# Block 0 of a two-block hybrid network as interleaved streams of steps, with a gathered top-1 FFN and a factored state-space decay

## The chip, the cores and the metric

One NeuronCore of a Trainium2 chip runs the whole network in one launch. The metric is the device time of a launch in microseconds (us), lower is better. The engines are PE (TensorE, matrix products, with PEld its weight loads), DVE (VectorE), ACT (ScalarE), POOL (GpSimd) and SP (SyncE, which only issues DMAs here). Every engine takes its instructions strictly in order; a DMA is issued by SP, ACT or POOL. All arithmetic is in fp32.

## The reference

The input is x, 4 sequences of 256 tokens with 256 features. Each of eight sub-layers adds to it:

```python
x = x + shift(layernorm(x))       # block 0, attention a: token shift, WKV recurrence
x = x + ffn0(layernorm(x))        # top-1 of 8 experts, 256 -> 256, with bias
x = x + ssm(layernorm(x))         # block 0, attention b: gated state space, 8 heads
x = x + ffn0(layernorm(x))        # the same weights again
x = x + attn_a(layernorm(x))      # block 1: grouped attention, 16 heads
x = x + ffn1(layernorm(x))        # top-4 of 32 experts, gated, inner width 96
x = x + attn_b(layernorm(x))      # the same with distance bias
x = x + ffn1(layernorm(x))
```

- shift mixes each token with the one before it in three ways (for k, v and r), projects each mix, runs the recurrences `a = e1*a + e2*v` and `b = e1*b + e2` over time, and projects `(a/b)*r`.
- ffn0 takes, for each token, the softmax over 8 router logits, the expert with the largest probability (the first one at a tie), and adds `prob * (W[expert] x + b[expert])`.
- ssm projects to gates, values h, B, C and step sizes dt, runs a causal convolution of width 4, and computes for each head `y[l] = sum over s<=l of (C[l].B[s]) * exp(sum of A*dt over s+1..l) * dt[s]*h[s]`, plus `D*h`; then the gate, a root-mean-square norm and an output projection. The kernels compute the sum over a whole sequence at once rather than in the reference's chunks.

## The kernel before

The 1024 tokens are two groups of 512 (two sequences each); a group is four tiles of 128 tokens, kept in SBUF as `x[g]`. Block 0 and block 1 are written differently.

**Block 0** is four plain functions called in turn: `l0_attn_a` (lines 155 to 233), `l0_ffn`, `l0_attn_b`, `l0_ffn`. Here the compiler's own scheduler orders the instructions of each engine. Each function goes over both groups before the next begins.

- `l0_attn_a`: for each group the norm, then three mixes (ACT L181, DVE L183). For each half e of the features: products pk, pv, pr; `top` and `low` (L206, L208) with their exponentials; four scans (L220, L222); a reciprocal of the denominator (DVE, `rb`, L225) and a multiply on POOL (L226); then the output products `po_a`, added to x.
- `l0_ffn` is dense. All eight experts are computed for all tokens and weighted by `comb`, which is zero but for the chosen one:

```python
for t in range(NT):
    for pr in range(E0 // 2):
        pe = mm_tile(...)
        project(pe, lambda c: xnT[:, c, t*P:(t+1)*P], lambda c: W[:, c, pr*512:(pr+1)*512])
        for h in range(2):     # x += pe[expert] * comb[expert], DVE L284
            ...
```

- `l0_attn_b`: projections and convolutions of both groups first (`pcv`, `pg`, `pd`), then the step sizes, then per group and sequence b eight heads. For each head POOL multiplies a triangular mask by `A*dt` (`au`, L394 and L396). PE sums it along time for three 128x128 blocks (`pS`, L400 to L402: the two diagonal blocks of the sequence and the block below them), ACT takes the exponential `L`, DVE multiplies by the masked `C.B` (`Gm`), and three products with the values give `pY` (L383 to L387). After the eight heads follows the tail of the sequence: add (`yf`, DVE L415), gate (POOL L417), squares, transposes `pyt`, output products `pob`, add to x.

**Block 1** is a dictionary of streams, each a Python generator that emits instructions and yields `(cost, wait)`. The function `weave` (L450) keeps a planner's clock, and always takes the next step of the ready stream with the lowest rank; a stream may name others that must have ended, and how long ago. It runs inside `tc.manual_schedule()`, so the order written is the order each engine gets. Its stream `a0` is the first attention of group 0, `a1` that of group 1; `r0`, `e0`, `c0` route, run the experts and combine. Routing sends normalised rows to slots in a DRAM buffer `sent` by indirect DMAs on POOL (L807); the experts fetch it tile by tile (SP), write `done` (SP), and the combine gathers rows back by indirect DMA (POOL, L890).

**Loads.** SP loads x of both groups, then all weights of block 0 and the attention weights of block 1. ACT loads the small ones, and writes zeros (`nil`) to `sent` and `done` (20 DMAs of 512 KB, L988 and L992). `negA`, an exponential of an input vector, is ACT's first computation (L293). After block 0 its weight pool closes; the FFN weights `gu` and `dw` of block 1 go to the same memory (issued from 369 us on), and constants of block 1's attention are built on POOL and DVE there (L1008 to L1068).

PSUM has eight banks: three "mm", two "st", two "sq", one "acc". In block 0 general products take turns on "mm" and "st"; in block 1 on "mm" alone.

Of the kernel before, what the change touches and what calls it, by code (L numbers as in the profile page):

```python
# [9 lines left out]
F32 = mybir.dt.float32  # L10
I32 = mybir.dt.int32
# [19 lines left out]
NH, HP, NS = 8, 64, 64  # L31
DI = NH * HP
# [5 lines left out]
def two_blocks(ctx: ExitStack, tc: tile.TileContext, a: dict, out: bass.AP):  # L38
# [33 lines left out]
    for g in range(NG):  # L72
        xg = const.tile([P, NT, D], F32, tag=f"x{g}", name=f"x{g}")
        for t in range(NT):
            nc.sync.dma_start(xg[:, t, :], xin[g, :, t, :])
        x.append(xg)

    ident = const.tile([P, P], F32, tag="ident", name="ident")
# [13 lines left out]
    for g in range(NG):  # L92
# [3 lines left out]
        sent_to.append(dram_disjoint_views(sent[g], NT * TOPK))  # L96

# [57 lines left out]
    def l0_attn_a(pool, wpool):  # L155
        wk, wv, wr, wo = (
            load(n, [P, NC, D], wpool, nc.scalar if i % 2 else nc.sync)
            for i, n in enumerate(("L0a_Wk", "L0a_Wv", "L0a_Wr", "L0a_Wo")))
        tm = vec[:, :, 0:3]
        bk, bv, br, u, w = (vec[:, :, i] for i in range(3, 8))  # L160
        omt = const.tile([P, NC, 3], F32, tag="omt", name="omt")
        nc.vector.tensor_scalar(omt, tm, -1.0, 1.0, ALU.mult, ALU.add)
        bku = const.tile([P, NC], F32, tag="bku", name="bku")
        nc.vector.tensor_tensor(bku, bk, u, ALU.add)
        bkuw = const.tile([P, NC], F32, tag="bkuw", name="bkuw")
        nc.vector.tensor_tensor(bkuw, bku, w, ALU.subtract)
        negw = const.tile([P, NC], F32, tag="negw", name="negw")
        nc.vector.tensor_scalar(negw, w, -1.0, None, ALU.mult)

        mixed = []  # L170
        for g in range(NG):
            xp = pool.tile([P, NC, 2, S + 1], F32, tag="xp", name=f"xp_{g}")
            nc.gpsimd.memset(xp[:, :, :, 0:1], 0.0)
            layernorm_T(g, f"a0_{g}", lambda c: xp[:, c, :, 1:S + 1])
            add_row(g, bo0)
            mix = []
            for j in range(3):
                m = pool.tile([P, NC, 2, S], F32, tag=f"mix{j}", name=f"mix{j}_{g}")
                for c in range(NC):
                    tmp = pool.tile([P, 2, S], F32, tag="mixtmp", name=f"mixtmp_{g}_{j}_{c}")  # L180
                    nc.scalar.activation(  # L181
# [1022 lines left out]
```

## Time and profile before

| | us |
|---|---|
| median of 14 runs (lowest, highest) | 1018.68 (1013.98, 1022.24) |
| the profiled execution | 1023.53 |
| its span, first to last instruction | 1021.8 |
| busy in the span: PE, PEld, DVE, ACT, POOL | 822.4, 509.4, 528.3, 251.8, 280.1 |
| shift stage of both groups ends at | 83 |
| first ffn0 ends at | 152 |
| ssm ends at | 300 |
| second ffn0 ends at | 370 |
| attention a of group 0 ends at | 459 |
| last product; last write | 988; 1022 |

All times are microseconds from the span's start. The groups of the profile give line, engine, operation, output<-inputs, shapes and count, then busy time and mean nanoseconds of one, then idle time of the engine just before them and what ended it. An fp32 product appears as two PE records, so x256 means 128 products. The granted clock is the share of full speed that PE was allowed.

### The profile page before, as it was taken

To read this page: it belongs to the slowest core of one execution; us is meant where nothing else is said; L and a number is where in the kernel's file an instruction comes from. 1 tells how busy PE (TensorE), PEld (TensorE's weight loads), DVE (VectorE), ACT (ScalarE), POOL (GpSimd) and SP (SyncE) were. 2 spreads that over 40 slices of the span, in tenths; PEclk is the share of its full clock that TensorE was granted. 3 is DMA by queue.
4 is the path that set the end of the run, shared out by engine and by line. 5 is a ranking of instruction groups with operands and counts; after the bars stand their busy time and mean duration, and the time that the engine had idled before them with its cause. 6 is when DMAs were issued, how large, how long until landed. Compare 5 with 4: busy or idle time off the path is not lost.

```text
span 1021.8 us, 10802 instructions
## 1 busy us (share of the span) xinstructions
PE 822.4 (80%) x3464; PEld 509.4 (50%) x3464; DVE 528.3 (52%) x1570; ACT 251.8 (25%) x470; POOL 280.1 (27%) x344
## 2 busy tenths in 40 slices
PE   3468999988889968888899776978888899776960
PEld 2234444577674434334337665854334337665850
DVE  5886665835336664526635423545736535423532
ACT  3410006722220002321235111212232234111210
POOL 3100000376530040020360324116220360324105
PEclk8688999998789978977799968988998799978995
DMA  8750000000000057000024435532000023435633
GB/s 281 271 185 1 1 0 1 1 1 1 1 1 0 1 159 213 1 0 21 32 81 116 144 105 184 165 114 62 11 1 0 32 80 96 145 113 173 188 110 99
DMA packets 61551, 81.49 MB, mean 80 GB/s; under 512 B 5928, under 2 KB 52528, under 8 KB 60976
## 3 DMA queue, kind: packets, MB, share of 16 engines
q1 hardware_dynamic: 43760, 52.48, 16.7%
q0 software_dynamic: 6144, 16.79, 5.2%
q10 hardware_dynamic: 11584, 11.46, 3.2%
q8 instruction: 30, 0.49, 0.2%
q14 instruction: 33, 0.27, 0.1%
HBM read 42.96 MB, written 37.75 MB: 79 GB/s over the span
## 4 chain that ended last, share of the span: by engine, by line
PE 59%; DVE 15%; issue 12%; POOL 6%; DMA 4%; ACT 2%; another core or an unknown queue 2%; POOLq 0%; ACTq 0%; SPq 0%; DVEq 0%
PE pe_f L142 11%; PE pgu_f L142 7%; PE py_f L865 3%; PE pST_a L601 3%; PE pS_a L559 3%; PE pcv L142 2%; PE pST_b L601 2%; PE pob L142 2%; DVE junk_a L570 2%; PE pS_b L559 2%; PE po_a L142 2%; DVE ye_f L873 2%; DVE junk_b L570 2%; POOL yb_f L890 2%
## 5 line engine op out<-in xcount | busy, mean ns | idle before, releaser
L142 PE MATMUL pgu_f<-gu,xT_f 128*128 128x192 f32 x512 | 109.9, 363 | 9.4 <-DVE ye_f L873 4.9
L142 PE MATMUL pe_f<-L0f_W_sb,xnT_f 128*128 128x512 f32 x256 | 115.7, 600 | 0.0
L142 PEld LDWEIGHTS pgu_f<-gu,xT_f 128*128 128x128 f32 x512 | 91.3, 208 | 21.0 <-DVE ye_f L873 17.1
L890 POOL DMA_INDIRECT yb_f<-done,bk_f x64 | 67.0, 1047 | 122.2 <-DMA xe_f<-sent 48.0
L807 POOL DMA_INDIRECT sent<-xn_f,to_f x64 | 63.0, 985 | 72.6 <-DVE full L794 55.4
L284 DVE SCALAR_TENSOR_TENSOR x<-pe_f,comb_f,x 128x256 f32<-128x256 f32 x128 | 61.9, 484 | 39.6 <-PE pe_f L142 36.2
L865 PE MATMUL py_f<-dw,hT_f 96*128 96x256 f32 x256 | 71.8, 407 | 3.4 <-issue 1.8
L142 PEld LDWEIGHTS pe_f<-L0f_W_sb,xnT_f 128*128 128x128 f32 x256 | 46.6, 190 | 53.9 <-issue 51.6
L869 DVE TENSOR_TENSOR he_f<-he_f,pgu_f 128x192 f32<-128x192 f32 x64 | 22.5, 352 | 83.7 <-ACT he_f L859 72.9
L570 DVE CUSTOM_DVE_ANT_0 junk_a<-pS_a,tri 128x128 f32<-128x128 f32 (+1 forms) x128 | 45.8, 358 | 33.1 <-PE pS_a L559 26.5
L570 DVE CUSTOM_DVE_ANT_0 junk_b<-pS_b,tri 128x128 f32<-128x128 f32 (+1 forms) x128 | 45.8, 358 | 29.6 <-PE pS_b L559 23.0
L842 ACT COPY xT_f<-px_f 128x512 f32<-128x512 f32 x64 | 37.2, 585 | 89.3 <-PE px_f L839 72.1
L873 DVE COPY ye_f<-py_f 128x512 f32<-128x512 f32 x64 | 44.2, 691 | 21.4 <-PE py_f L865 7.1
L865 PEld LDWEIGHTS py_f<-dw,hT_f 96*128 96x128 f32 x256 | 49.9, 204 | 10.5 <-issue 2.3
L839 PE MATMUL px_f<-ident,xe_f 128*128 128x128 f32 x256 | 42.2, 294 | 12.3 <-DMA xe_f<-sent 10.1
L859 ACT ACTIVATE he_f<-pgu_f 128x192 f32<-128x192 f32 x64 | 21.1, 330 | 119.4 <-PE pgu_f L142 82.0
L881 DVE SCALAR_TENSOR_TENSOR x<-yb_f,wt_f,x 128x256 f32<-128x256 f32 x64 | 30.9, 484 | 37.3 <-DMA yb_f<-done,bk_f 37.1
L394 POOL TENSOR_SCALAR au<-m,dtad 128x256 f32<-128x256 f32 x32 | 31.0, 968 | 63.6 <-DVE dtad L350 38.3
L848 PE MATMUL ph_f<-ident,he_f 128*96 128x128 f32 x128 | 26.6, 291 | 26.9 <-DVE he_f L869 24.5
L608 POOL TENSOR_SCALAR_AFFINE_SELECT pT_a<-pT_a 128x512 f32<-128x512 f32 x32 | 19.7, 637 | 94.8 <-ACT pT_a L606 94.4
L839 PEld LDWEIGHTS px_f<-ident,xe_f 128*128 128x128 f32 x256 | 34.3, 153 | 22.6 <-issue 13.1
L606 ACT ACTIVATE pT_a<-pST_a 128x512 f32<-128x512 f32 x48 | 26.5, 595 | 73.0 <-PE pST_a L601 72.0
(297 smaller groups left out, 1456.0 us busy)
## 6 DMA issues: line engine op xcount, KB each, us to landing
xe_f<-sent SPq DMA_DIRECT2D x64, 256.0 KB, 2.7
done<-ye_f SPq DMA_DIRECT2D x64, 256.0 KB, 2.1
sent<-nil ACTq DMA_DIRECT2D x18, 512.0 KB, 3.1
gu<-in_L1f_gate SPq DMA_DIRECT2D x4, 768.0 KB, 18.1
gu<-in_L1f_up SPq DMA_DIRECT2D x4, 768.0 KB
dw<-in_L1f_down SPq DMA_DIRECT2D x4, 768.0 KB
L0f_W_sb<-in_L0f_W SPq DMA_DIRECT2D x4, 512.0 KB, 7.8
L0b_in_sb<-in_L0b_in SPq DMA_DIRECT2D x1, 1160.0 KB
```

Of the source, the lines that this page charges most:

```text
L142: nc.tensor.matmul(dst, w(c), rhs(c), start=(c == 0), stop=(c == n - 1))
L284: nc.vector.scalar_tensor_tensor(x[g][:, t, :], pe[:, h * D:(h + 1) * D], comb[:, t, e:e + 1], x[g][:, t, :], ALU.mult, ALU.add)
L394: nc.gpsimd.tensor_scalar(au[:, :S], m384[:, :S], ad[:, 2 * b, h:h + 1], None, ALU.mult)
L559: nc.tensor.matmul(both[r][:, at:at + 2 * w].rearrange("p (s k) -> p s k", s=2), qT[rows, c, q0:q0 + P], kb[rows, 2 * r:2 * r + 2, b * S:b ...
L570: nc.vector.tensor_tensor_reduce(out=junk[:, :w], in0=both[r][:, at:at + w], in1=tri[:, S - w:], scale=1.0, scalar=NEG, op0=ALU.add, op1=A ...
L601: nc.tensor.matmul(pS, kb[rows, s, k0:k0 + P], qm[rows].rearrange("p c q -> p (c q)"), start=True, stop=True)
L807: nc.gpsimd.indirect_dma_start(out=sent_to[g][t * TOPK + j], out_offset=bass.IndirectOffsetOnAxis(ap=to[:, t, j:j + 1], axis=0), in_=xn[:, ...
L839: nc.tensor.transpose(px[:, j * P:(j + 1) * P], xe[q][:, k, c * P:(c + 1) * P], ident)
L842: nc.scalar.copy(xT[q].rearrange("p k c t -> p (k c t)"), px)
L865: nc.tensor.matmul(py[:, k * D:(k + 1) * D], hT[q][:, k, :], dw[:, 2 * q + k, :], start=True, stop=True)
L873: nc.vector.tensor_copy(ye.rearrange("p k d -> p (k d)"), py)
L890: nc.gpsimd.indirect_dma_start(out=yb, out_offset=None, in_=done[g], in_offset=bass.IndirectOffsetOnAxis(ap=back[:, t, j:j + 1], axis=0), ...
```

## The change

Block 0 is rewritten as streams too, and the whole kernel runs under `tc.manual_schedule()` with one planner clock. All its general products now use the three "mm" banks.

**Streams.** A is the shift stage of a group, R a route, X the fetch of extra experts' weights, E the experts, C the combine, S the state space; T, Y, G, D are R, X, E, C of the second FFN. The number is the rank, the last dictionary says after which streams, and how long after:

```diff
+        streams = {
+            "A0": (2, shift_mix(0, a0, shift), {}),
+            "A1": (3, shift_mix(1, a0, shift), {}),
+            "R0": (0, first_route("f00", 0, f0, first, ways0[0]), {"A0": 0.5}),
+            "R1": (0, first_route("f00", 1, f0, first, ways0[0]), {"A1": 0.5}),
+            "E0": (1, first_experts("f00", 0, f0, W, bias, eb, ways0[0]), {"R0": 1.5}),
+            "E1": (1, first_experts("f00", 1, f0, W, bias, eb, ways0[0]), {"R1": 1.5, "E0": 0.0}),
+            "X0": (0, first_extra("f00", 0, f0, first, ways0[0]), {"R0": 0.0}),
+            "X1": (0, first_extra("f00", 1, f0, first, ways0[0]), {"R1": 0.0}),
+            "C0": (0, first_combine("f00", 0, f0, ways0[0]), {"E0": 3.0}),
+            "C1": (0, first_combine("f00", 1, f0, ways0[0]), {"E1": 3.0}),
+            "fix": (0, second_fix(), {"A0": 0.0}),
+        }
+        weave(streams, ("A0", "A1"))
...
+            "S0": (4, state_space(0, b0, space), {"C0": 0.5}),
+            "S1": (5, state_space(1, b0, space), {"C1": 0.5, "S0": 0.0}),
+            "T0": (0, first_route("f01", 0, f0, first, ways0[1]), {"S0": 0.5}),
+            "G0": (1, first_experts("f01", 0, f0, W, bias, eb, ways0[1]), {"T0": 1.5, "E1": 0.0}),
+            "Y0": (0, first_extra("f01", 0, f0, first, ways0[1]), {"T0": 0.0}),
+            "D0": (0, first_combine("f01", 0, f0, ways0[1]), {"G0": 3.0}),
+        weave(streams, ("S1", "fix"))
...
+            "T1": (0, first_route("f01", 1, f0, first, ways0[1]), {"S1": 0.5}),
+            "G1": (1, first_experts("f01", 1, f0, W, bias, eb, ways0[1]), {"T1": 1.5, "G0": 0.0}),
+            "Y1": (0, first_extra("f01", 1, f0, first, ways0[1]), {"T1": 0.0}),
+            "D1": (0, first_combine("f01", 1, f0, ways0[1]), {"G1": 3.0}),
+            "a0": (2, attention("a1", 0, *attn_a), {"D0": 0.5}),
+        weave(streams, ("D1",))
+        early0.close()
+        w1 = ctx.enter_context(tc.tile_pool(name="w1", bufs=1, side="right"))
...                          # loads of gu and dw; then the streams of block 1 as before
+            "na": (3, norm_steps(1, "a1_1", early[0]), {"D1": 0.5}),
```

`weave(left, until)` keeps its clock between calls and stops when the named streams have ended. The pool `b0` of the state space takes the memory of the shift stage; `gu` and `dw` take that of block 0's weights.

**The FFN on slots.** Each expert has 128 slots per group, and three further tiles of 128 take the overflow of whichever experts have more than 128 tokens: 11 tiles. `first_route` computes router logits, the chosen expert, each token's rank within it (by products with triangular and all-ones matrices), then the slot on DVE in some 30 small operations, and scatters four tiles of rows:

```diff
+        for t in range(NT):
+            nc.gpsimd.indirect_dma_start(
+                out=first_to[g][t],
+                out_offset=bass.IndirectOffsetOnAxis(ap=to[:, t:t + 1], axis=0),
+                in_=xn[:, t, :], in_offset=None, bounds_check=EXTRA + 3 * P - 1,
+                oob_is_err=False)
+            yield 0.0, 1.28
```

`first_extra` finds which experts own the three extra tiles, and gathers their weights by six indirect DMAs (128 rows of 1 KB each). `first_experts` goes over six pairs of tiles, the last with one:

```diff
+                px = mm_tile(f"px_{name}_{i}")
+                for j in range(k * NC):
+                    nc.tensor.transpose(
+                        px[:, j * P:(j + 1) * P],
+                        xe[i][:, j // NC, (j % NC) * P:(j % NC + 1) * P], ident)
...
+                nc.scalar.copy(
+                    xT[i][:, :k].rearrange("p k c t -> p (k c t)"), px[:, :k * NC * P])
...
+                if q < 4:
+                    for j, e in enumerate(pairs[q]):
+                        project(py[:, j * D:(j + 1) * D], lambda c: xT[q][:, j, c, :],
+                                lambda c: W[:, c, e * D:(e + 1) * D])
+                    nc.vector.tensor_tensor(
+                        yf_, py[:, :k * D], bias[:, 2 * q * D:(2 * q + k) * D], ALU.add)
+                else:                # extra tiles: bias by a product with "chose", weights xw
...
+                    nc.scalar.copy(yf_, py[:, :k * D])
+                nc.sync.dma_start(first_done[g][...], ye[:, :k])
```

`first_combine` gathers four tiles of rows from `first_done` by indirect DMA on POOL and adds them to x with the gate, four DVE operations.

**The state space.** One generator per group. The two diagonal blocks keep masked sums, exponentials and products, now two heads at a time; the block below them is split into a factor of the earlier half (`reach[:, t]`, applied to the values: `left`) and one of the later half (`reach[:, NT + 2b + 1]`, applied to the product):

```diff
+            pS = mm_tile(f"pS_{g}_{b}_{h}")
+            nc.tensor.matmul(pS, strict, au.pop(k).rearrange("p h i l -> p (h i l)"),
+                             start=True, stop=True)
...
+            for h in (h0, h0 + 1):
+                hs = slice(h * HP, (h + 1) * HP)
+                for i in range(2):
+                    nc.tensor.matmul(pY[b][i][:, hs], L[k][:, h - h0, i, :],
+                                     hdt[2 * b + i][:, h, :], start=True, stop=True)
...
+        def between(b):
+            pO = bank("acc", f"pO_{g}_{b}")
+            nc.tensor.matmul(pO, Gm[b][:, 1, :], left[b].rearrange("p h q -> p (h q)"),
+                             start=True, stop=True)
```

The eight jobs (two sequences, four pairs of heads) form one loop; the gate, transposes and output products of sequence 0 are steps put between the jobs of sequence 1.

**The shift stage.** The same operations as steps; the scans of the denominator come before those of the numerator, and the output factor pr comes after both halves.

**Start and constants.** SP loads x of group 0, two weights, then x of group 1. On ACT, ahead of its first computation, come two zero fills of the slot buffers (1.44 MB each) and a broadcast of the expert biases (1 MB); DVE's multiply of `negA` is written ahead of all norms:

```diff
+        for g in range(NG):
+            nc.scalar.dma_start(
+                first_sent[g].rearrange("(p k) d -> p k d", k=E0 + 3),
+                nil.unsqueeze(1).to_broadcast([P, E0 + 3, D]))
...
+        nc.scalar.dma_start(
+            bias, a["L0f_b"].rearrange("e d -> (e d)").partition_broadcast(P))
...
+        nc.scalar.activation(negA, alog, AF.Exp)
+        nc.vector.tensor_scalar(negA, negA, -1.0, None, ALU.mult)
```

`second_fix` is a stream of rank 0: the 20 zero fills for block 1, one step each, and the constants of its attention, after A0. The loads of `gu` and `dw` are issued after D1's last step.

## The prediction

> **What bounds the kernel now.** I read the page's strip, then a table of stages, then the chain of the worst stages. A row is start:end, its length, busy us of PE, PEld, DVE, ACT and POOL, granted clock, DMA share, GB/s. In order: shift stage, first FFN, state space (two halves), second FFN, first attention of group 0.
>
> ```profile
> 12.00:83.00 71.00, 43.26 (x98) 24.24 (x99) 55.08 (x82) 21.91 (x30) 13.73 (x14) 0.74 0.65 228
> 83.00:152.00 69.00, 68.52 (x203) 32.09 (x202) 44.11 (x119) 3.75 (x8) 2.02 (x2) 1.00 0.00 0
> 152.00:197.00 45.00, 42.83 (x133) 20.17 (x132) 29.74 (x58) 29.90 (x45) 5.03 (x7) 0.96 0.00 1
> 197.00:300.00 103.00, 88.99 (x527) 78.15 (x526) 45.16 (x97) 32.15 (x71) 60.80 (x72) 0.85 0.00 1
> 300.00:370.00 70.00, 68.01 (x201) 31.61 (x198) 44.17 (x119) 3.75 (x8) 3.33 (x9) 1.00 0.00 1
> 370.00:459.00 89.00, 73.20 (x269) 33.85 (x270) 40.37 (x165) 22.87 (x42) 21.78 (x47) 0.81 0.37 107
> ```
>
> Both FFNs are pure PE at full clock. The shift stage is DVE (55 of 71). The state space has PE 89 of 103 busy at clock 0.85, so it has holes; its chain of waits shows where:
>
> ```profile
> 275.82 0.43 PE pob L142 x2
> ...
> 288.74 0.22 PE pY L387 x2
> ...
> 289.32 0.70 DVE yf L415
> 290.10 2.50 POOL yf L417 x2
> 292.64 1.54 PE pyt L430 x6
> 294.18 5.83 PE pob L142 x16
> ```
>
> Eight heads run from 277.1 to 289.3; then a serial tail to 300.0 costs 10.7 us, and the same matmul that took 0.43 a pair at 275.8 now takes 5.83/8 = 0.73, the PE having idled. There are four such tails. The costly groups:
>
> ```profile
> L142 PE MATMUL pe_f<-L0f_W_sb,xnT_f 128*128 128x512 f32 x256 | 115.7, 600 | 0.0
> L225 DVE RECIPROCAL rb<-sb 128x512 f32<-128x512 f32 x4 | 13.4, 3349 | 0.1
> L890 POOL DMA_INDIRECT yb_f<-done,bk_f x64 | 67.0, 1047 | 122.2 <-DMA xe_f<-sent 48.0
> ```
>
> Block 0 ends near 370; group 0's first attention ends at 459; 1021.8 - 459 = 563 us follow. The planner emits that remainder in the same order of steps before and after, so I carry 563 over and price the road to "a0 ends".
>
> **Start.** The shift's first normalised tile is written at 11.68. Its timeline (start, duration):
>
> ```profile
> 9.53 0.44 ACTq L65 DMA_DIRECT2D L0b_norm_sb<-in_L0b_norm  x1
> 9.99 1.28 ACT L293 ACT_TABLE_LOAD   x1 [9.99 <-DMA L0f_wg_sb<-in_L0f_wg]
> 11.29 0.21 ACT L293 ACTIVATE negA<-row 128x8 f32<-128x8 f32 x1
> ```
>
> ACT reaches that exponential only after issuing its DMAs. The change puts three large ones ahead of it (two zero fills of 1.44 MB, one bias broadcast of 1 MB), and, the order being manual, the DVE's negA multiply now stands ahead of both groups' statistics. Issue of one existing 512 KB zero fill costs 0.52 to 1.25, mean 1.06 in a burst of five. New issue time: at least 3x0.52 = 1.6, at most 2x2.75x1.25+1 = 8; I take 6, by the burst. So negA is done at 17.5; eight pairs of statistics (0.42+0.18, 4.6 together) then give the first normalised tile at about 22 (18 to 26): +10. Group 1's x moves behind two weight loads on SP; they issue in 0.33 each and x is wanted only at 20: nothing.
>
> **Shift stage.** Same operations. DVE from there: 8 norms 3.3, mixes 10.5, top/low 6.1, scans 11.6, ev 3, reciprocals 13.4, yT 3, output adds 3.4 = 54; plus group 0's routing, norm 4.2 and some 30 tiny ones at 0.16 = 5. The first 8.3 us (norm to first projection) hold 5 of DVE work, and group 0's chain runs nearly alone, with some 7 of exposed waits: 54+9+3+7 = 73, I take 74 (68 to 78). Group 1's shift ends at 96, its routing of group 0 with it.
>
> **FFN.** Removed: 137 us of dense PE. Added per group and pass: 11 tiles of two transposes (0.60 per four, so 0.30) and two 256-column products (0.44 each at full clock, as in py x4 at 0.88) = 13, plus three small bias products 1.3: 14.3; transposes, logits and rank products 1.2+1.9+1 = 4. Four times 18.3 is 73: PE work falls by 64. But each pass is now a chain through DRAM: scatter, fetch, products, store, gather. Indirect DMAs step at 1.28 to 1.31 on POOL; a fetch lands in 2.7, a store in 2.1, a gather in 3.3 to 3.6.
>
> First pass, between the stages: group 1's statistics end at 98.4; the planner puts its rsqrt (1.05) before group 0's fourth scatter, which issues at 100.6 and lands at 103 (2.5, between store and gather); the fetch lands at 106. Products 14.3, plus 4.5 for group 1's logits and ranks among them: 125; store 128.5; four gathers alternating with group 1's weight gathers, all queued on POOL: 138.5. Group 1 scatters until 121.5, fetches by 127, multiplies until 146. State space of group 0 is queued on DVE behind group 1's evictions (141), and its norm takes 6.4; its first PE work comes at about 150. So 54 us here (46 to 62) against 69: group 0's add is hardly hidden, since S0 waits for C0.
>
> **State space.** Per group: projections and convolutions 45/2 = 22.5. Per head before: 1.55 (pS 0.94, pY 0.61). After, two heads share one 512-column product (0.88) and need four pY (0.88): 1.76, eight times 14.1 against 24.8. Added: one 512-column product per sequence (1.8) and 0.4 of decay products; unchanged pG 1.7, transposes 1.8. First sequence's tail now lies among the heads: 3.5+1.2 of PE. Filling the first heads 3, last tail 10.7. Sum 22.5+14.1+2.2+3.5+4.7+3+10.7 = 61 (56 to 66). POOL's masked products fall from 32x(0.97+0.66) = 52 to about 16x1.26 = 20, the row of the 128x512 gate multiply; it no longer binds. S1 cannot start before S0 ends; its norm exposes 7. Beside S1 lies group 0's second pass: 18.3 of PE, its waits hidden by S1's convolutions. 150+61+7+61+18 = 297.
>
> **a0.** Norm 7: the constants that kept POOL busy and held rstd_a until 375 are built earlier, a gain of 4.5. From pk (381.4) to 458.9 it took 77.5, and group 1's second pass adds 18.3: 297+7+78+18 = 400 (390 to 412). The load of gu and dw (9.4 MB at 285 to 303 GB/s, 32 us) now waits for D1, around 370, and is first used some 80 us later: nothing, but up to 32 if that cover went. The other twenty zero fills take ACT 13 to 25 us of issue, covered by its slack (85 busy of 370).
>
> **Stalls.** 56 indirect DMAs are new. During such a burst of 16, engines stop on something that is not a kernel operation:
>
> ```profile
> ACT he_f L859 <- remote: 6.4, 1, 6.4
> ```
>
> I see about 10 us lost in that burst, 5 in the next: 0.3 to 0.6 each would be 17 to 34, but those were denser and beside 16 fetches; bounds 0 to 20, I take 8. a0 ends at 408.
>
> [...]
>
> [...]
>
> **Sum.** 408+563 = 971 span, plus the 1.7 by which this execution (1023.5) exceeded its span: 973. The median of the runs is 4.9 under that execution, so I expect 968; against 1018.7 that is -50.
>
> **Rivals.**
> *The chains are not hidden.* All engines run the planner's fixed order, so a gather or fetch that lands later than planned blocks PE, DVE or POOL with state-space or attention work behind it. For: ACT and DVE stopping 4 to 6 us in the burst. Against: 23 us of convolutions to hide under. If both second passes expose a chain like the first's group 0 (106 to 138 plus routing, some 30 us each, 60 for both), 968+60 = 1028. It decides from 50 us of exposed waits on.
> *Fewer waits than I gave.* The start isn't held (-8), stalls are 0 (-8), the first pass takes 46 (-8) and the state space 56 twice (-10): 934. For: PE-dense parts run at 1.00. Against: the shift's clock of 0.74.
> *The overlap exists in the order of issue only:* S0 waits for group 1's evictions and for its buffers, S1 for S0, so the groups still follow one another. Most of this is already in my sum; another 7 to 10 us at both handovers and 62 in the first pass: 968+26 = 994.
>
> **How the numbers follow.** Forecast (950 to 985) 0.45; fewer waits (below 950) 0.20; partial overlap (985 to 1016) 0.22; chains exposed (above 1020) 0.11; between them 0.02. Range 928 to 1012: below it lies 0.07 and above it 0.13. A measurement can tell 0.2% from no change, so 1016.6 to 1020.7 is "same". Faster 0.87, same 0.02, slower 0.11.
>
> **What would show it.** First xn at 22 and not 12; pe_f gone, py/px groups of 44 tiles in all; PE busy near 740; S0's first product near 150; two tails of about 10 us rather than four; a0 ending near 408 with the same 563 behind it. I am wrong if PE has idle stretches above 10 us ended by a DMA inside S1 or a0, if the first pass exceeds 62, or if the remainder changes its length.

## The result: slower by 0.9%, and the profile after

The changed kernel takes 1027.67 us (median of 10 runs, 1021.23 to 1031.40) against 1017.99 for the kernel before: a ratio of 1.0093, 95% interval 1.0077 to 1.0109. The forecast was 968 us. The page of its profiled execution:

```profile
span 1027.4 us, 10502 instructions
...
PE 762.2 (74%) x3264; PEld 488.1 (48%) x3264; DVE 501.3 (49%) x1556; ACT 257.4 (25%) x481; POOL 312.1 (30%) x361
...
PE 45%; issue 21%; DVE 15%; DMA 6%; POOL 5%; ACT 3%; another core or an unknown queue 3%; SPq 0%; POOLq 0%; ACTq 0%; DVEq 0%
```

PE is busy 60 us less than before (762 against 822), as a gain of the size forecast would need, and the span is longer all the same. The stages, in the columns of the first table above (start, the first FFN pass, state space of group 0, then group 1's with the second pass of group 0, attention of group 0 with the second pass of group 1, the remainder):

```profile
0.00:33.00 33.00, 0.00 (x0) 0.00 (x0) 5.43 (x30) 1.49 (x2) 4.80 (x25) 1.00 0.95 345
33.00:122.00 89.00, 52.28 (x126) 27.66 (x126) 61.55 (x109) 23.53 (x33) 15.81 (x11) 0.77 0.18 61
122.00:181.00 59.00, 42.92 (x183) 33.30 (x183) 20.66 (x79) 10.64 (x21) 23.62 (x23) 0.77 0.68 222
181.00:251.00 70.00, 57.28 (x216) 34.60 (x216) 40.17 (x71) 25.62 (x48) 29.96 (x51) 0.88 0.11 34
251.00:375.00 124.00, 95.87 (x359) 65.52 (x360) 63.78 (x157) 34.46 (x64) 39.36 (x35) 0.79 0.12 39
375.00:469.00 94.00, 81.96 (x338) 41.43 (x337) 45.52 (x202) 25.78 (x49) 27.67 (x32) 0.92 0.50 151
469.00:1027.00 558.00, 431.90 (x2046) 285.63 (x2044) 264.19 (x912) 135.83 (x265) 170.88 (x184) 0.87 0.30 95
```

Up to the end of the first attention PE works 330 us (second to sixth row); the rows of before gave 385 from 12 to 459. So 55 us of work are gone, but PE's idle time in that stretch rose from 74 (12 of the start included) to 139. The remainder is 558 us against the 563 that I carried over. The whole question is where 65 us of new idle time come from.

The start shows at once. ACT's own instructions there:

```profile
5.90 4.55 ACTq L1203 DMA_DIRECT2D fsent<-nil  x2
13.38 0.57 ACTq L66 DMA_DIRECT2D L0f_wg_sb<-in_L0f_wg  x1
14.42 1.18 ACTq L66 DMA_DIRECT2D L0f_b_sb<-in_L0f_b  x1
18.72 0.36 ACTq L1209 DMA_DIRECT2D bias<-in_L0f_b  x1
26.08 0.33 ACTq L66 DMA_DIRECT2D L0b_conv_sb<-in_L0b_conv  x1
26.45 0.44 ACTq L66 DMA_DIRECT2D L0b_norm_sb<-in_L0b_norm  x1
26.93 1.28 ACT L1271 ACT_TABLE_LOAD   x1 [26.93 <-DMA fsent<-nil]
28.22 0.21 ACT L1271 ACTIVATE negA<-row 128x8 f32<-128x8 f32 x1
```

The two zero fills cost 4.55 to issue, within my bounds. But between the end of one issue and the start of the next ACT then stands 2.9, 0.5, 3.1 and 7.0 us, 13.5 in all, and the profile ends this idle time with the DMA `fsent<-nil`. In these 33 us the DMA engines are nearly always busy (first row of the table: share 0.95, 345 GB/s). The exponential comes at 28.2 instead of 11.3. On DVE the multiply of `negA` starts at 28.46, after 23.85 us of waiting for it, and the first statistics, written behind it, at 28.55; the first normalised tile at 33.2.

The FFN's products on PE, all four passes (busy us, mean ns of one):

```profile
L150 PE MATMUL py_f<-L0f_W_sb,xT_f 128*128 128x256 f32 x128 | 36.2, 434 | 1.0 <-ACT xT_f L468 1.0
...
L464 PE MATMUL px_f<-ident,xe_f 128*128 128x128 f32 x88 | 16.4, 324 | 14.6 <-DMA xe_f<-fsent 10.9 <-issue 2.1 <-DVE x L512 1.6
...
L150 PE MATMUL pl_f<-L0f_wg_sb,xnT_f 128*128 128x8 f32 x64 | 13.9, 355 | 0.6 <-ACT xnT_f L215 0.6
L490 PE MATMUL py_f<-xw_f,xT_f 128*128 128x256 f32 x48 | 13.6, 405 | 0.0
...
L210 PE MATMUL pt_f<-ident,xn_f 128*128 128x128 f32 x32 | 9.5, 449 | 15.9 <-DVE xn_f L202 15.0 <-DVE low L273 0.9
...
L487 PE MATMUL py_f<-L0f_b_sb,chose_f 8*128 8x256 f32 x24 | 8.3, 426 | 0.0
```

py and px come to 74.5, or 18.6 a pass, where I had 14.3; logits, transposes and 5.4 of rank products to 28.8, or 7.2, where I had 4. A pass is 25.8 us of PE work on average instead of 18.3; with overlapping records counted once, the two first passes have 26.1 each, the second pass of group 0 25.7 and that of group 1 22.6.

### The profile page after: what moved, and what is told of

Read it like the earlier page. It is cut to its first block, busy times and chain, and to the rows that moved or that the text cites. A ratio compares the mean times of both kernels' runs of the same rounds, so it can differ in the third digit from the quotient of the medians.

```text
span 1027.4 us, 10502 instructions
## 1 busy us (share of the span) xinstructions
PE 762.2 (74%) x3264; PEld 488.1 (48%) x3264; DVE 501.3 (49%) x1556; ACT 257.4 (25%) x481; POOL 312.1 (30%) x361
## 4 chain that ended last, share of the span: by engine, by line
PE 45%; issue 21%; DVE 15%; DMA 6%; POOL 5%; ACT 3%; another core or an unknown queue 3%; SPq 0%; POOLq 0%; ACTq 0%; DVEq 0%
PE pgu_f L150 6%; PE py_f L150 3%; PE py_f L1111 3%; PE pST_a L847 3%; PE pS_a L805 2%; DVE junk_a L816 2%; PE pST_b L847 2%; DVE cv L537 2%; PE pS_b L805 2%; DVE ye_f L1119 2%; PE pob L150 2%; DVE junk_b L816 2%; DMA fsent<-nil 2%; PE pq_a L150 1%
## 5 line engine op out<-in xcount | busy, mean ns | idle before, releaser
L150 PEld LDWEIGHTS pgu_f<-gu,xT_f 128*128 128x128 f32 x512 | 89.8, 205 | 19.9 <-DVE ye_f L1119 16.1
L1115 DVE TENSOR_TENSOR he_f<-he_f,pgu_f 128x192 f32<-128x192 f32 x64 | 22.5, 352 | 87.6 <-ACT he_f L1105 76.2
L1111 PEld LDWEIGHTS py_f<-dw,hT_f 96*128 96x128 f32 x256 | 49.5, 203 | 13.3 <-issue 3.5
L852 ACT ACTIVATE pT_b<-pST_b 128x512 f32<-128x512 f32 x48 | 26.3, 595 | 73.0 <-PE pST_b L847 72.3
L847 PE MATMUL pST_a<-qm_a,kb_a 64*128 64x512 f32 x96 | 34.2, 693 | 8.1 <-DVE qm_a L832 5.3
L847 PE MATMUL pST_b<-qm_b,kb_b 64*128 64x512 f32 x96 | 34.8, 714 | 6.2 <-DVE qm_b L832 3.4
L805 PE MATMUL pS_b<-kb_b,qT_b 64*128 64x256 f32 (+1 forms) x128 | 36.6, 594 | 3.5 <-DVE nmx L816 3.4
L210 PE MATMUL pt_a<-ident,xn_a 128*128 128x128 f32 x32 | 8.6, 423 | 40.6 <-DVE xn_a L202 40.6
```

The source lines that it names most:

```text
L150: nc.tensor.matmul(dst, w(c), rhs(c), start=(c == 0), stop=(c == n - 1))
L805: nc.tensor.matmul(both[r][:, at:at + 2 * w].rearrange("p (s k) -> p s k", s=2), qT[rows, c, q0:q0 + P], kb[rows, 2 * r:2 * r + 2, b * S:b ...
L847: nc.tensor.matmul(pS, kb[rows, s, k0:k0 + P], qm[rows].rearrange("p c q -> p (c q)"), start=True, stop=True)
L852: nc.scalar.activation(pT.rearrange("p c q -> p (c q)"), pS, AF.Exp)
L1111: nc.tensor.matmul(py[:, k * D:(k + 1) * D], hT[q][:, k, :], dw[:, 2 * q + k, :], start=True, stop=True)
```

## Experiments

Five groups of runs (e1 to e4; base_after and e5 to e7; e8 to e11; e12 to e15; e16) each share a chip and its runs of the kernel before. The five chips are of two kinds: the kernel before takes 984.7 to 985.5 us on three of them and 1017.5 to 1017.9 on two (and 1017.99 where the changed kernel was first measured), so only ratios are compared across. Inside block 0 the two kinds agree: e2, which up to the end of group 1's state space S1 is the changed kernel, starts its first output product `pob` at 236.5 on a faster chip, against 236.6 and 237.0 (base_after) on slower ones. So I use a mark there: the start of the last record of `pk` of group 1's attention, which ends the line of its group.

```profile
L150 PE MATMUL pk_a<-xnT_a,L1a_Wk_sb x8: 592/826/1201, 374.5 to 470.5; 128*128 128x512 f32 x8
```

That is 470.5 here, 461.3 for the kernel before. Each mark comes from one trace. The changed kernel gave 470.5 and 474.0, e1 and e8, the same kernel, 454.2 and 452.4; and S1's last `pob` starts at 354.5 in e2, but at 358.8 and 361.2 in the two traces of the changed kernel, from the same instructions. Differences of some 4 us or less in the mark are not told apart, and a larger one needs a second sign. The start edit alone was not run on a slower chip, so what e5, e6, e7, e12, e13 and e15 gain or lose over it rests on the mark.

| run | edit | ratio to before [95%] | mark |
|---|---|---|---|
| base_after | none (another slower chip) | 1.0101 [1.0066, 1.0136] | 474.0 |
| e1 / e8 | start | 0.9859 [0.9809, 0.9908] / 0.9899 [0.9858, 0.9940] | 454.2 / 452.4 |
| e2 / e3 | second pass of group 1 / 0 left out, old start | 0.9833 [0.9766, 0.9900] / 0.9814 [0.9753, 0.9875] | 441.9 / 448.5 |
| e4 | start, FFN dense | 1.0248 [1.0194, 1.0303] | 487.4 |
| e5 | start, shift order | 0.9946 [0.9919, 0.9974] | 452.4 |
| e6 | start, Silu late | 0.9897 [0.9854, 0.9940] | 447.0 |
| e7 | start, decay not factored | 1.0103 [1.0066, 1.0140] | 464.3 |
| e9 | start, S1 cut in two | 0.9917 [0.9886, 0.9948] | 459.5 |
| e10 | start, T1 behind a0 | 1.0136 [1.0103, 1.0168] | 474.3 |
| e11 | start, fills later | 0.9883 [0.9836, 0.9930] | 456.8 |
| e12 | start, norms ahead | 0.9848 [0.9810, 0.9887] | 445.0 |
| e13 | start, constants first | 0.9957 [0.9927, 0.9986] | 458.6 |
| e15 | start, Silu, norms, constants | 0.9685 [0.9646, 0.9723] | 430.8 |
| e14 | all five: start, shift order, Silu, norms, constants | 0.9612 [0.9570, 0.9653] | 428.0 |
| e16 | all but the constants | 0.9619 [0.9584, 0.9654] | 426.3 |

e1 to e4, e8 to e11 and e16 ran on faster chips, the others on slower ones.

**The start (e1, e8), and the changed kernel as it is on another slower chip (base_after).**

```diff
-        for g in range(NG):
-            nc.scalar.dma_start(first_sent[g]..., nil...)     # ahead of wg
...
-        nc.scalar.dma_start(bias, ...)
...                                  # behind the load of L1f_router
+        nc.sync.dma_start(bias, ...)
+        for g in range(NG):
+            nc.sync.dma_start(first_sent[g]..., nil...)
```

> The changed kernel with one edit: the two zero fills of the slot buffers and the bias broadcast are issued by SP behind all weight loads instead of by ACT ahead of its first computation. Theory (ACT stands in DMA issue until 26.9 us and everything behind it is serial): negA near 10, first normalised tile near 13 to 15 instead of 33.2, time down by 15 to 21, about 1009. Rival (the later chains set the pace, or the same bytes only block something else): down by 5 or less.

> The changed kernel as it is, beside the next three on the same chip. If its ratio to the kernel before is a property of the two kernels, 1.009 again; e1_start then is worth 2.3%.

> The start edit alone (zero fills and bias broadcast on SP behind the weight loads), once more, as the measure for the three others on their chip. Theory (the stall of ACT at the start is a plain delay of 16 us): ratio to the kernel before lower than that of the changed kernel by 0.016, so about 0.994 where the changed kernel had 1.010; the first attention of group 1 begins near 454. Rival (the 0.986 of the first time was the chip's): 1.00 or more.

The first normalised tile moves from 33.2 to 16.6, and the mark by 16 to 22: the stall was a plain delay at the head of the chain. Beside e2 and e3, which have the old start on e1's chip, the first `pob` comes 17 to 19 earlier (217.7 against 236.5 and 234.9). With this one edit the change is 1.0 to 1.4% faster than the kernel before on those chips.

**What the second passes and the slots are worth (e2, e3, e4).** e2 has no T1, Y1, G1 and D1, e3 no T0, Y0, G0 and D0, so one group lacks the second FFN (the norm of group 1's attention then follows D0, group 0's attention S0); e4 has a start as in e1 (there are no slot buffers to fill and no bias to broadcast) and, in place of R, X, E and C, a stream of dense steps as in the kernel before.

```diff
-            "T1": ..., "G1": ..., "Y1": ..., "D1": ...        # e2; T0 to D0 in e3
+            "F0": (1, dense_steps("f00", 0, f0, first, W, eb), {"A0": 0.5}),   # e4
```

> The changed kernel without group 1's second top-1 FFN (streams T1, Y1, G1, D1 left out; its part of the result is missing). If its waits are hidden beside the first attention, it costs its PE work, 18 to 20: about 1008. If its chain through DRAM is exposed, 30 or more: below 998.

> The changed kernel without group 0's second top-1 FFN (streams T0, Y0, G0, D0 left out; its part of the result is missing). Hidden beside the second state space: 18 to 20 less, about 1008. Exposed, as the length of the second state space (99 us against 70 for the first) suggests: 27 to 30 less, about 999.

> Streams and the factored state space kept, the start as in e1_start (no slot buffers to fill), but the FFN dense as in the kernel before: all eight experts for every token, no scatter or gather, written as steps. If the slots pay for themselves, it is slower than e1_start by up to the 64 us of PE work that they save, some 40 after overlap with the shift stage's idle PE. If the chains through DRAM eat that, it is within 15 us of e1_start, or faster.

e3 moves the mark by 22 to 26 and e2 by 29 to 32; by the ratios (1.0093 or 1.0101, less 0.9833 and 0.9814, of 984.7) a second pass costs 26 and 28 us, give or take 7, not 18.3. Of e2's gain 4 to 7 us are there before its edit begins (S1's last `pob`, above); ahead of that, the routing's logits at the first handover took 2.17 us at a granted clock of 0.86 instead of 3.42 at 0.50. From that `pob` to the mark e2 takes 87.4 us and the changed kernel 111.7, so 24 us less, of which 21.5 are PE's busy time (70.5 against 91.9). From the first `pob` to S1's last, where group 0's pass lies, e3 takes 97.9 instead of 122.3, with 78.8 of PE instead of 97.6. So 19 to 21 of 24 us are products and some 3 to 6 are waits: most of the chain through DRAM is hidden, the products are not. Dense is 0.039 of the time before, or 38 us, slower than slots: the slots do pay.

**The shift order (e5).** More declared wait behind the exponentials, `pr` a step apart from `yT`, and a buffer for each group, so that group 1's products fill group 0's waits.

```diff
-            return pool.tile([P, 2, S], F32, tag=n, ...)
+            return pool.tile([P, 2, S], F32, tag=f"{n}{g}", ..., bufs=2 if n == "sa" else 1)
...
             nc.scalar.activation(top, top, AF.Exp, ...)
-            yield 1.75, 0.0
+            yield 1.75, 2.8
```

> e1_start, with the shift stage's steps given waits for the exponentials and one pool tag per group, so that group 1's DVE work is put into group 0's waits, and with yT as a step of its own behind its product. DVE stands idle about 25 of the 89 us of this stage in the changed kernel. If those gaps are what the stage lost against my 74, it ends 8 or more earlier and the time falls by about as much against e1_start. If the road to the first experts is set by when group 0's shift ends, which comes later here, nothing is gained or a few us are lost.

The last `po_a` of the shift moves from 103.3 to 91.3, so the stage is 12 us shorter; but the first `px` of the first pass only from 113.9 to 109.7 and the state space's first product from 163.1 to 159.6, and the mark by 0 to 2. By the trace the pass now starts from group 0's routing, some 30 small DVE steps among group 1's work: its slots are ready at 94.9 instead of 99.9, and the scatters follow.

**Silu late (e6).**

```diff
+        def bent(j):
+            nc.scalar.activation(hT[j], hT[j], AF.Silu)
         for i in range(1, 6):
             conv(order[i])
+            bent(order[i - 1])
```

> e1_start, with each convolution's Silu issued on ACT behind the next convolution's first operation instead of ahead of it. In the changed kernel a convolution and a gate take 4.2 us, the sum of 0.77 on ACT, 2.31 on DVE, and 0.54 and 0.5 on ACT, in series. If that ACT order is the bound, the period falls to PE's 3.6 and five convolutions in two groups give 5 to 7 us. If the three PSUM banks are the bound, nothing.

The chain of waits in the changed kernel, one convolution and the start of the next (start, us, what):

```profile
196.48 0.68 ACT cv L533
...
197.18 0.76 DVE cv L537
...
197.96 0.76 DVE cv L537
...
198.74 0.76 DVE cv L537
...
199.58 0.63 ACT cv L540
200.21 0.48 ACT sg L547
200.69 0.68 ACT cv L533
```

ACT opens a convolution (L533), DVE adds three taps, and ACT closes it with Silu (L540). The next opening (200.69) stands behind the Silu (199.58) and a gate (200.21), and the Silu waits for the taps, the last of which starts at 198.74: 4.2 us a turn, in series. PE has 3.4 us of products in it. With the Silu one convolution later, the same stretch of e6 is a row of products:

```profile
175.47 1.98 PE pg L150 x4
177.45 1.72 PE pcv L150 x4
```

From the first `pcv` to the last `pG` of the group it takes 23.0 us (166.3 to 189.3) instead of 28.8 (183.5 to 212.3), or 27.4 in e1 and e8. The whole state space of group 0, from its first `pd` to the end of its last `pob`, takes 62.7 instead of 70.8 in e1, and the mark moves by 5 to 7. The rival, that the three PSUM banks set the pace, is out.

The kernel before had this order already. Its ACT, as the compiler's scheduler arranged it, opens the second convolution ahead of the first Silu, and the third ahead of the second (L306 opens, L313 is Silu):

```profile
155.07 0.78 ACT L306 ACTIVATE cv<-pcv,L0b_conv_sb 128x512 f32<-128x512 f32 x1 [1.65 <-PE pcv L142]
156.72 0.78 ACT L306 ACTIVATE cv<-pcv,L0b_conv_sb 128x512 f32<-128x512 f32 x1 [0.88 <-PE pcv L142]
158.42 1.28 ACT L313 ACT_TABLE_LOAD   x1 [0.92 <-DVE cv L310]
159.71 0.63 ACT L313 ACTIVATE cv<-cv 128x512 f32<-128x512 f32 x1
160.25 0.76 ACT L306 ACTIVATE cv<-pcv,L0b_conv_sb 128x512 f32<-128x512 f32 x1
160.91 0.62 ACT L313 ACTIVATE cv<-cv 128x512 f32<-128x512 f32 x1
161.43 1.43 ACT L306 ACTIVATE cv<-pcv,L0b_conv_sb 128x512 f32<-128x512 f32 x2
```

All products of group 0's projections lie between 152.99 and 172.6 there, those of group 1 begin at 175.35: the two groups did not overlap.

**The decay not factored (e7).** Single heads, the block below the diagonal by masked sums again, no `left`, `off` and `pO`.

```diff
-                nc.tensor.matmul(pS, strict, au..., start=True, stop=True)   # two heads
+                nc.tensor.matmul(pS[:, :S], strict, t[:, :S], start=True, stop=False)
+                nc.tensor.matmul(pS[:, P:S], every, t[:, S:], start=False, stop=True)
+                nc.tensor.matmul(pS[:, S:S + P], strict, t[:, S:], start=True, stop=True)
```

> e1_start with the decay of the state space undone: per head three blocks, two POOL products, three sums, one exponential and three value products, as in the kernel before; streams and slots stay. By PE a head takes 1.55 instead of 0.88: 32 heads 21 us, less 4 for the factor's own products: 17 slower than e1_start. If POOL's 1.63 per head takes over, up to 25. If the tails and the chains set the pace, under 8.

The mark is 10 to 12 later than with e1: the factoring saves 5 to 6 us a group. I had 24.8 - 14.1 - 2.2 = 8.5.

**S1 cut in two (e9).** Norm, projections and convolutions of group 1 as a stream of rank 3 beside group 0's heads; gates, heads and tail stay behind.

```diff
+            "H1": (3, part(half[1], False, 1.2), {"C1": 0.5}),
-            "S1": (5, state_space(1, b0, space), {"C1": 0.5, "S0": 0.0}),
+            "S1": (5, part(half[1], False), {"H1": 0.0, "S0": 0.0}),
```

> On top of the start edit, group 1's state space is cut in two: its norm, projections and convolutions come beside group 0's heads, its gates, heads and tail stay behind group 0. Theory (the state space of a group is a series of short steps on ACT and DVE in which PE waits, and since group 1 follows group 0 nothing of the state space fills that): the handover of 9 us and some 30 us of convolutions leave the stretch behind group 0; group 0's heads stretch by the 20 us of PE work that comes in. Net 12 to 20 us off the mark where group 1's attention begins (454 to about 438), ratio 0.012 to 0.02 under the start edit's. Rival (PE's clock and the second pass's own chain set the length): the mark moves by less than 4 us, because group 0's combine, a chain of about 70 us behind its state space, then ends last.

A miss: the mark is 5 to 7 later. The table loads of ACT up to 480 us are one candidate:

```profile
L540 ACT ACT_TABLE_LOAD x5 | 6.4, 1283 | 12.6 <-DVE cv L537 12.6
...
L651 ACT ACT_TABLE_LOAD x4 | 5.1, 1283 | 0.1
```

Silu (L540) of one stream and the decay's Exp (L651) of the other alternate, and nine table loads of 1.28 us stand at these two lines. In all, e8 has 11 loads up to there, e9 has 19. The output products begin 37 us later than in e8 (254.7, 217.8), and what follows up to group 1's last one is only 33 shorter (89.9, 122.6). The convolutions hold ACT and DVE wherever they are put; that group 0's heads pay for it there is what I read from it, and no run isolates the table loads. Nor does one isolate the buffers: to make room, e9 gives the heads' tiles 4 buffers instead of 5 (`hdt`, `hd`) and 3 instead of 4 (`L`).

**T1 behind a0, fills later, constants first (e10, e11, e13).** One line each: the rank of T1 from 0 to 2.5; `fix` after E1 instead of A0; in `second_fix` the constants ahead of the fills.

> On top of the start edit, the second routing of group 1 gets a rank behind the attention of group 0 instead of ahead of it. Theory (8 us of its norm, transposes and logits stand in front of the attention's first product and nothing fills them): the first pk comes 6 to 8 us earlier, and group 1's attention begins 5 to 8 us earlier; the loads of gu and dw begin 15 to 35 us later, which is hidden. Rival (in-order engines meet the same instructions later): 0, or the later loads show as a wait in the experts of block 1, up to 20 us slower.

> On top of the start edit, the 20 zero fills for block 1 and its constants come after the experts of group 1's first pass instead of after group 0's shift. Theory (the fills share the DMA engines with the first pass's scatters, fetches and gathers): the first pass's products start 3 to 5 us earlier, all of block 0 with them. Rival (the pass is set by its routing's small steps and the fills only take what is free): 0 to 1 us, or up to 5 us slower because the constants on POOL and DVE then fall into the state space.

> On top of the start edit, the constants of block 1's attention are built before the 20 zero fills instead of behind them. Theory (2.5 us of memsets and selects on POOL stand between the masked products of group 0's first heads, on the chain of waits): group 0's state space ends 2 to 3 us earlier, everything behind it too. Rival (the masked products have slack): 0; or the constants now stand in front of the scatters of group 0's first pass on POOL: up to 4 us slower.

None of the three theories held. e10 brings `pk` from 356.1 to 352.0 and then loses 22 us at the mark. Among the waits of PE between 330 and 480 us:

```profile
PE pt_f L210 <- DVE xn_f L202: 14.5, 2, 13.3
```

The 13.3 us lie at the end of group 0's attention (454.0 to 467.3), just ahead of the mark: the transposes of block 1's first routing wait there until group 1's second pass has stored its last slots, gathered, added (462.2) and been followed by two norms. That is the pass's chain through DRAM in the open, now that the pass ends last; it is not the wait for the loads of `gu` and `dw` that the rival named. e11 changes nothing that the ratio can tell; the mark is 3 to 4 later. e13 was to test the changed kernel's chain, which passes through those memsets (`nmx`, from 218.88 on, between two masked products `au`). But from `pG` to the first `yf` it takes 16.1 us there (212.3 to 228.4), 16.1 in e8, and 17.8 in e13 (198.9 to 216.8), where no constant is in the way: the constants did not set this stretch. And the memsets now stand in the shift stage, whose last `po_a` moves to 107.7 (103.2 in e8, 104.9 in e12 on e13's chip); the mark is 4 to 6 later, a little more than the rival's 4.

**Norms ahead (e12).**

```diff
+            "n1": (3, norm_steps(1, "b0_1", ahead[1]), {"C1": 0.5}),
-            "S1": (5, state_space(1, b0, space), {"C1": 0.5, "S0": 0.0}),
+            "S1": (5, state_space(1, b0, space, ahead[1]), {"n1": 0.0, "S0": 0.0}),
+            "n0": (3, norm_steps(0, "a1_0", ahead[0]), {"D0": 0.5}),
```

> On top of the start edit, the norm of group 1's state space and the norm of group 0's attention become streams of their own, written beside the stretch before, so that neither stands at a handover. Theory (at each handover PE waits for two norms, that of the next stage and that of the second routing, 9 and 15 us long): each handover shrinks by 5 to 7 us, the first product of the attention (pk, 356) comes at 344 to 348 and that of group 1's attention (452 to 454) at 440 to 444; ratio 0.010 to 0.014 under the start edit's. Rival (the routing's own norm and logits stand there anyway, in order on DVE and PE): at most 4 us in all.

A handover is the stretch on PE from the end of a stage's last output product to the next stage's first projection. At the first one of the changed kernel, from group 0's state space to group 1's, it is 13.4 us (250.2 to 263.6, `pd`). The chain at the second, whose last output product ends at 359.2:

```profile
364.45 1.26 POOL rstd_f L109
...
365.74 2.50 DVE xn_f L202
...
368.29 2.30 PE pt_f L210 x8
370.58 0.85 PE pt_a L210 x4
371.43 3.21 PE pl_f L150 x16
374.65 1.91 PE pk_a L150 x2
```

Two norms, one behind the other, then T1's logits, all ahead of `pk`: 15.4 us (359.2 to 374.65). In e12 the last record of `pob` starts at 345.8 and `pk` at 346.1; the mark is 7 to 9 earlier.

The clock has a part in it. The 16 records of the routing's eight logit products, which take 3.21 at both handovers of the changed kernel, take 1.84 behind the first one of e12, where they follow products:

```profile
255.17 3.75 PE pg L150 x4
258.92 1.84 PE pl_f L150 x16
```

PE's granted clock is 0.65 from 359 to 374 in the changed kernel and 0.50 during its logits at both handovers, against 0.95 during those of e12; the ratio of the two times is 1.74. What sets the clock no run shows.

**All together (e14, e15, e16).**

> Start edit, shift order, Silu late, norms ahead and constants first together. If the pieces are plain delays in one chain they add: 2 + 7 + 8 + 2 = 19 us before the mark where group 1's attention begins (453 to about 434), ratio 0.97 to 0.975 on a chip where the start edit gives 0.988. If they take the same slack from each other: 440 to 447.

> Start edit, Silu late, norms ahead and constants first, without the shift order. If the first pass's chain through DRAM and not the shift stage sets when group 0's state space starts, this is within 3 us of the kernel with all five; if the shift stage counts, 4 to 10 us slower.

> The kernel with all five edits less one: the constants of block 1 stay behind the zero fills, since building them first alone moved group 1's attention from 452 to 459. If that loss is also in the kernel with all five (428), this one reaches the mark at 421 to 425, ratio 0.953 to 0.958; if the shift order had absorbed it, 427 to 431 and 0.959 to 0.965.

The edits do more together than alone: by the marks one by one, 1 + 6 + 8 off 453 would leave 438, and e16 has 426.3; its ratio agrees, 0.024 to 0.028 under e1 and e8 on chips of its kind. The shift order, worth 0 to 2 alone, seems worth 2.8 in e14 against e15, whose state space starts at 166.6 instead of 163.2; but e15's trace alone has a 5.0 us wait of ACT in the first pass (152.3 to 157.3) of the unnamed kind described at the end, so the marks don't settle it. By the ratios it would be 7 us, with intervals that touch. Leaving the constants out gave 1.7 at the mark and nothing in the ratio, so e16's finer guess (421 to 425) missed. e14 on a slower chip takes 978.87 us, e16 on a faster one 946.96: both beat the kernel before by 0.038. The stages of e16, cut as above:

```profile
0.00:17.00 17.00, 0.00 (x0) 0.00 (x0) 5.84 (x32) 1.49 (x2) 4.84 (x26) 1.00 0.74 211
17.00:97.00 80.00, 52.25 (x126) 28.63 (x126) 61.91 (x111) 23.75 (x33) 12.90 (x8) 0.81 0.42 148
97.00:163.00 66.00, 47.29 (x199) 36.12 (x200) 20.32 (x76) 11.00 (x21) 27.64 (x27) 0.76 0.70 234
163.00:232.00 69.00, 61.12 (x228) 37.14 (x228) 42.94 (x89) 28.14 (x52) 31.11 (x51) 0.86 0.07 21
232.00:329.00 97.00, 80.17 (x317) 51.58 (x316) 55.50 (x130) 33.65 (x61) 37.83 (x33) 0.89 0.16 49
329.00:425.00 96.00, 81.82 (x354) 44.71 (x353) 46.86 (x211) 26.89 (x51) 28.50 (x33) 0.88 0.36 111
```

PE works 323 us up to 425, and idles 102 instead of 139.

## Why the prediction was wrong

The stages beside the prediction's steps (us; e16 is the same computation, better ordered; the second pass of group 0 lies in the fifth row, group 1's in the sixth):

| | forecast | changed kernel | e16 |
|---|---|---|---|
| first normalised tile | 22 | 33.2 | 16.8 |
| shift stage | 74 | 88.5 | 75.8 |
| first FFN pass, to the first `pd` | 54 | 59.2 | 67.6 |
| S0, to its last `pob` | 61 | 69.3 | 68.6 |
| norm, S1 and second pass | 86 | 109.0 | 96.5 |
| norm, attention, second pass, stalls | 111 | 110.2 | 99.9 |
| a0 ends | 408 | 469.4 | 425.2 |

The rows add up to the 61 us by which a0 ends late: 11 + 14.5 + 5 + 8 + 23 - 1. No single one explains them. Four edits of order (e16) give back 44; the 17 that stay are of the kind of the products below, which no edit touched.

**Start: +11, mis-sized.** I priced the issue instructions (at most 8 us) and took ACT to be free once they were out. The trace has ACT stand another 13.5 us between its issues; e1 and e8, with the first tile 16.6 us and the mark 16 to 22 us earlier, show that all of it went into the time.

**Shift: +14.5, mis-sized, but not where it hurt most.** The 74 were nearly right for a good order (76 in e5 and e16). The planner's order let group 1's long DVE steps stand before group 0's. Taking the 12 us out gained 2 at most by itself. In e5 the routing's slots are ready only 5 us earlier: of the shift stage's end and the routing's, I had only the first as a cause.

**First pass: +5.** Mis-sized with the PE term below. e16's 67.6 begins at an earlier shift end; its state space starts at 160.2, e1's at 163.1.

**S0: +8, the failed step.** I took 22.5 for projections and convolutions from half of the old stage, and let the streams run at the old pace. That pace needs ACT to open a convolution before it closes the one ahead of it, as the compiler's scheduler had arranged. The order written for the streams closes first, so ACT and DVE run in series: 31.4 from the first `pd` to the last `pG`, 9 more than I had, while the rest of S0 takes 37.9 where I had 38. e6, which only changes that order, has 23.0 between first `pcv` and `pG` instead of 27.4 to 28.8, and 62.7 for S0 where I had 61. The row that I needed was ACT's and DVE's time for one convolution in the order written, not PE's busy time. (e16's S0 is longer again, 68.6; it also has the norm of group 1's state space beside it, with which e12's takes 73.3.)

**Norm, S1 and second pass: +23,** the largest row, are 6 in the handover and 7 in the products of the pass. The other 9 or 10 lie in S1 itself, and no run explains them: e6's order, which shortens S0 by 8, shortens S1 by 2 (from its first `pd` to the end of its last `pob`, 91.7 against 93.5 in e1).

**POOL "no longer binds" held** (e13): the constants in the chain cost nothing that taking them out gives back. My gain of 4.5 from them at a0's norm came, in that `rstd` no longer waits for POOL, but a second norm took its place.

**Handovers: 7 each, measured 13 and 15.** I counted the norm of the next stage, not that the routing of rank 0 puts a second norm and eight logit products, at a granted clock of 0.50, into the same gap. e12 shows 7 to 9 us of it.

**Second passes: 24 in their own stretches, 26 and 28 by the ratios, instead of 18.3.** Mis-sized mostly by the products: 1.13 for a tile's two products (36.2 over 32 tiles) instead of 0.88, 1.83 with bias for an extra tile, logits at 0.355 a record. I took the rows for full clock; the stretches of the changed kernel that hold the passes have granted clocks of 0.77 (first pass), 0.79 and 0.92 (second passes). Over four passes this is 30 us of PE work; PE busy is 762, where I said 740.

**What held.** The remainder (558 for 563); the factoring in sign; the dense work removed (e4); no idle stretch over 10 us ended by a DMA inside S1 or a0. The 8 us of stalls in block 0 aren't there: the trace of the changed kernel has no such wait up to a0's end. The waits that I took the 8 from stand in every trace of the slower chips and in none of the faster ones, so they don't come with indirect DMAs as such.

**Rivals.** The time fell on "the chains are not hidden" (1028), but not by its mechanism: it wanted some 30 us of waits in each second pass, and e2 and e3 find a whole pass to take 24 in its stretch, of which 3 to 6 are waits. Only e10 shows such a chain in the open, for 13 us. Nearer is "the overlap exists in the order of issue only", which gave the two handovers 7 to 10 each beyond my 7; they cost 6 and 8 beyond it. It was priced at +26 and had no place for the start, the convolutions or the products.

**What stays open.** Why the edits add up to more than their sum, beyond that each frees the same DVE and ACT queues; what makes up the 9 or 10 us that S1 takes beyond the forecast, its handover and the pass's products; and what part of a pass's 1.13 a tile is the clock and what is waiting between the records.

## What to carry to other kernels

When stages are turned into streams, price each stage by the longest series of dependent steps that its engines run in the order now written, not by what the stage took before: the compiler's scheduler may have hidden those steps in each other, as it had the convolutions here (written in that order again, in e6, they take 23.0 us instead of 27.4 to 28.8), and the old trace shows in which order. Put no large DMA on the queue of an engine that has an early step on the chain; here such a stall held the first normalised tile back by 16.6 us and the mark by 16 to 22. Before a reordered version is given up, look at each handover for norms and routings that the planner's costs don't know of: four edits of order turned +0.9% into -3.8% here.

## What the runs showed of the hardware

- With large DMAs on its queue, ACT stood for 16 us without computing anything: behind 4.55 us of issue for two 1.44 MB fills came gaps of 0.5 to 7.0 us ahead of the next four issues (13.5 us in all).
- The two kinds of chip differ by 3.3% on the kernel before, and the difference lies in block 1: behind the mark follow 551 to 561 us in every trace on a slower chip and 514 to 521 in every one on a faster. e14 and e16, for instance, reach the mark at 428.0 and 426.3; then follow 982.3 - 428.0 = 554 and 944.7 - 426.3 = 518 us. The traces on the slower chips have waits that the profile ends with `remote`, mostly in the experts of block 1; in e14 (in all, times, longest):

```profile
ACT he_f L1111 <- remote: 19.5, 4, 6.4
```

  e16, like every trace on a faster chip, has no such wait. That is 19.5 us of waiting beside a difference of 36; what ACT waits for the trace doesn't say.
- The same instructions met different clocks: up to the end of S1 e2 is the changed kernel, yet its 16 records of logits at the first handover took 2.17 us (granted clock 0.86) instead of 3.42 (0.50), and S1 ended 4 to 7 us earlier.
- With Silu and Exp of two streams alternating on ACT, e9 has 19 table loads up to 480 us where e8 has 11; each takes 1.28 us.
